# The excite of a dynamic convolution moved from TensorE to VectorE, in a two-layer convolution kernel

## The chip, the cores and the metric

The kernel runs on one core of a Trainium2 chip. The metric is the device time of one execution in microseconds, as the median of several runs. Before the change it is 3594.07 us (three runs, 3593.32 to 3596.56).

## What is computed

The input x is 16 images of 192 channels and 64 by 64 pixels, in fp32. A first layer (a layer norm, projections, depthwise convolutions, scans in four directions, a batch norm over all images, and a two-layer perceptron with residuals) gives an image of the same shape. The second layer, which the change is about, takes a mean of every channel, works four convolution taps per image and channel out of these means, and applies them:

```python
def _L1_conv_ref(x, w1, gamma, beta, running_mean, running_var, w2, b2, bias):
    ...
    b, c, h, w = x.shape
    pooled = x.mean(axis=(2, 3))
    t = pooled @ w1.T
    t = gamma * (t - running_mean) * jax.lax.rsqrt(running_var + EPS) + beta
    t = jax.nn.relu(t)
    wt = t @ w2.T + b2
    wt = wt.reshape(b * DIM, 1, K, K) * jnp.tile(MASK, (b, 1, 1, 1))
    out = jax.lax.conv_general_dilated(x.reshape(1, b * c, h, w), wt, window_strides=(1, 1), padding=((1, 1), (1, 1)), feature_group_count=b * DIM, dimension_numbers=('NCHW', 'OIHW', 'NCHW'))
    out = out + jnp.tile(bias, (b,))[None, :, None, None]
    return out.reshape(b, c, h, w)
```

`pooled @ w1.T` (192 to 48 values), the normalisation and the relu are called the squeeze here, `t @ w2.T + b2` (48 values to taps) the excite. The mask leaves four of the nine taps.

## The kernel before

The program writes the order of each engine's instructions out by hand: an engine works its instructions in the order in which the Python calls them, and waits where a tile that it needs isn't ready. It has three stages.

The first stage (lines 250 to 595) norms and projects the pixels, 64 chunks of 9.4 us on TensorE. Small jobs are hung on single chunks with `beside(n, ...)`: chunks 40 to 44 load weights (`load_weights`, among them `w1t` and `w2t`, the weights of squeeze and excite), and chunk 50 runs `squeeze_scale`, which works out the factor `s1` of the normalisation and divides `w1t` by the number of pixels.

The second stage (lines 598 to 806) runs over pairs of channels: `depthwise`, `scans`, `local`, `vertical`, `gate`. Its loop begins at k = −2; there TensorE first does `hidden_bias` (line 141: 18 products with one column, tile `pb_h`) and then `depthwise(0)` (line 629, tile `ps_d`). The tile `stats` takes the batch-norm sums from `gate(0)` on, and nothing uses it earlier.

The third stage (lines 810 to 1376) takes two images at a time, a pair, in 8 chunks of 512 pixels: 64 iterations of the loop at line 1256. Of 128 partitions the first 64 hold the one image and the others the other, with the 192 channels in three groups t of 64. In an iteration, TensorE does the first layer of the perceptron of chunk n (`first`, line 996), the means and the output projection for later chunks (`mean`, `out_quarters`, `out_columns`, lines 935, 899, 906), and the second layer (`second`, `seven`, `last_tile`, with line 851 for all their products). VectorE adds the results to the image (`residual`, `onto`), ScalarE does the activations, GpSimd the sums of operands that `seven` needs (`differences`).

Where a pair has ended (`ended`, the first iteration of the next pair, eight times in all), the taps are worked out: `pooled` adds the channel sums up (line 1109), `squeeze` multiplies them with `w1t` on TensorE (line 1115, tile `ps_t`: 48 partitions, one column per image) and normalises on VectorE (lines 1117 and 1118), and `excite` makes the taps with 24 products of one column each (through `both`, line 851, tile `ps_k`) and adds b2 on VectorE (line 1128). `squeeze` is called between the two halves of the output projection, `excite` between two steps of `second`. From the next lines on, `begin` and `piece` apply the taps: the first on ScalarE (line 1138), three on VectorE (line 65), in pieces spread over the next pair's iterations. After the last pair there is nothing to spread them over: squeeze, excite, diagonal matrices of the taps (line 1348), and the convolution on TensorE, ScalarE and VectorE at once (`dynamic_last`) follow each other.

PSUM is handed out in pools: `f1` (two tiles of two banks), `f2` (three of one bank) and `a` (one bank). `ps_t` is of `f1`, `ps_k` of `a`, the accumulators of `second` are of `f2` and `f1`.

Of the kernel before, what the change touches and what calls it, by code (L numbers as in the profile page):

```python
# [31 lines left out]
CH = 512  # L32
# [4 lines left out]
NG = HW // GR  # L37
NFC = 6
RED = 48
NTAP = 4  # L40
# [15 lines left out]
def conv_block_kernel(ctx: ExitStack, tc: tile.TileContext, x, prm, w_in, w_out, w_fc1, b_fc1, w_fc2, w1, bn1, w2, out):  # L56
    nc = tc.nc
    n_img_all = x.shape[0]
    n_pairs = n_img_all // 2
# [3 lines left out]
    HALF = (slice(0, 64), slice(64, 128))  # L63
# [23 lines left out]
    pt3 = cp.tile([128, 3, NPRM], F32, tag="pt3", name="pt3")  # L87
    eps5 = cp.tile([128, 1], F32, tag="eps5", name="eps5")
    eps6 = cp.tile([128, 1], F32, tag="eps6", name="eps6")
    ident = cp.tile([128, 128], F32, tag="ident", name="ident")  # L90


    k2 = ctx.enter_context(tc.tile_pool(name="k2", bufs=1))
# [6 lines left out]
    wf2 = place[:, 0:NFC * C].rearrange("p (m c) -> p m c", m=NFC)  # L100
    bf1 = k2.tile([128, NFC], F32, tag="bf1", name="bf1")
    w1t = k2.tile([128, 3, RED], F32, tag="w1t", name="w1t")
    w2t = k2.tile([RED, NTAP, C], F32, tag="w2t", name="w2t")
    b1 = k2.tile([RED, 4], F32, tag="b1", name="b1")
    s1 = k2.tile([RED, 1], F32, tag="s1", name="s1")

    mean64 = k2.tile([128, 64], F32, tag="mean64", name="mean64")

# [22 lines left out]
    def squeeze_scale():  # L131
        nc.scalar.activation(s1, b1[:, 3:4], AF.Sqrt, bias=eps5[0:RED])
        nc.vector.reciprocal(s1, s1)
        nc.vector.tensor_mul(s1, s1, b1[:, 0:1])

        nc.vector.tensor_scalar_mul(w1t, w1t, 1.0 / NPIX)

    def hidden_bias(pb):
        for m in range(NFC):
            for t in range(3):  # L140
                nc.tensor.matmul(pb[:, m:m + 1], wf1[0:64, t, 128 * m:128 * m + 128],  # L141
                                 pt3[0:64, t, LN2B:LN2B + 1], start=(t == 0), stop=(t == 2))
        nc.vector.tensor_add(bf1, bf1, pb[:, 0:NFC])
# [18 lines left out]
    ce = early.enter_context(tc.tile_pool(name="early", bufs=1))  # L162

    SB_ = 2 * 2 * C * BR
    mid = ce.tile([128, SB_], F32, tag="mid", name="mid")
    ones = ce.tile([128, 128], F32, tag="ones", name="ones")
    pv = ce.tile([128, 2, NPRM], F32, tag="pv", name="pv")


# [1 line left out]
    dec_b = ce.tile([128, 2, C // 2], F32, tag="dec_b", name="dec_b")  # L171
    bias_q = ce.tile([128, 3, C // 2], F32, tag="bias_q", name="bias_q")
    stats = ce.tile([128, C, 6], F32, tag="stats", name="stats")

    mask = ce.tile([128, 2, 1, HW], F32, tag="mask", name="mask")

# [73 lines left out]
    with ExitStack() as stage:  # L250
# [291 lines left out]
        for dst, src in ((pt3, prm), (w0, w_in)):  # L542
            v = src.rearrange("(t p) n -> p t n", p=64)
# [54 lines left out]
    with ExitStack() as stage:  # L598
# [168 lines left out]
        for k in range(-2, n_bp + 1):  # L767
            if 0 <= k + 1 < n_bp:
                tables(k + 1)
            if k >= 1:  # L770
                vertical(k - 1)
                gate(k - 1)
                g, c = divmod(k, hp_)
                if c == 0 and 0 < g < NCG - 1:
                    load_lm(g + 1)
                if c == 0 and g == 3:
                    load_weights(2)
                if c == 0 and g + 2 < NCG:
                    load_pg(g + 2)
                if c == hp_ - 2 and g + 2 < NCG:  # L780
                    load_dm(g + 2)
            if 0 <= k + 1 < n_bp:
                scans(k + 1)
            if k == -2:
                hidden_bias(psb.tile([128, 2, CH], F32, tag="l", name="pb_h")[:, 0])
            if k + 2 < n_bp:
                depthwise(k + 2)
            if 0 <= k < n_bp:
                local(k)
                sigmoid(k)  # L790
            if k in (1, 3, 5):
                scale_hidden(k // 2)
            if k == n_bp - hp_:

                load_y(0, y_low, (nc.sync,), (0, 1))
                load_x2(0)
                load_x2(1)
            if k == n_bp - hp_ // 2:
                load_y(0, y_low, (nc.sync,), (2,), LASTC)
# [48 lines left out]
    def both(ps, w, rhs, start, stop, **kw):  # L848

        for i, q in enumerate(HALF):  # L850
            nc.tensor.matmul(ps[q], w(i), rhs(i), start=start, stop=stop, **kw)  # L851
# [259 lines left out]
    def squeeze(p):  # L1111
        s = pst[p]
        pt = ps2.tile([128, 2, CH], F32, tag="f1", name="ps_t", bufs=2)[:, 0]
        for t in range(3):
            nc.tensor.matmul(pt[0:RED, 0:2], w1t[:, t], pool2[:, t], start=(t == 0), stop=(t == 2))
        red = hp2.tile([RED, 2], F32, tag="red2", name="red2")
        nc.vector.tensor_scalar(red, pt[0:RED, 0:2], b1[:, 2:3], s1, ALU.subtract, ALU.mult)
        nc.vector.tensor_scalar(red, red, b1[:, 1:2], 0.0, ALU.add, ALU.max)
        s["red"] = red

    def excite(p):
        s = pst[p]
        pk = ps2.tile([128, 3, NTAP, 1], F32, tag="a", name="ps_k")
        for t in range(3):
            for k in range(NTAP):
                both(pk[:, t, k], lambda i: w2t[:, k, 64 * t:64 * t + 64], lambda i: s["red"][:, i:i + 1], True, True)
        taps = hp2.tile([128, 3, NTAP], F32, tag="taps", name="taps")
        nc.vector.tensor_add(taps, pk[:, :, :, 0], pt3[:, :, B2:B2 + NTAP])
        s["taps"] = taps

    def dynamic(p, g, t):
# [124 lines left out]
    for n in range(n_ch + 1):  # L1256
        p, c = divmod(n, NCH)
        ended = p - 1 if n and c == 0 else None
        at(final, n - 1)
        if ended is not None:  # L1260
            pooled(ended)
            if ended == n_pairs - 1:
                idle(1)
        if n == 0:
            nc.vector.memset(pool2, 0.0)
        if n == 1:
            load_y(6, ys[3], (nc.sync,))
# [36 lines left out]
        at(first, n, NPS + 2)  # L1304
        at(differences, n, 2, 2)
        po = []
        if n + 2 < n_ch:

            own = [ps2.tile([128, CH], F32, tag="f2", name="ps_o1", bufs=3)[:, 0:HCH],
                   ps2.tile([128, CH], F32, tag="a", name="ps_o1")[:, 0:HCH]]  # L1310
            pair = ps2.tile([128, 2, CH], F32, tag="f1", name="ps_o", bufs=2)
            po = [[pair[:, wh, 0:HCH] for wh in range(2)], own, [pair[:, wh, HCH:CH] for wh in range(2)]]
            out_quarters(n + 2, 1, po[1], True)
        if n + 1 < n_ch:
            st[n + 1]["pw"] = two_banks("ps_v")
            mean(n + 1, st[n + 1]["pw"], "sq")
        at(load, n + 3)
        if po:
            for t in (0, 2):
                out_quarters(n + 2, t, po[t], True, t < 2)  # L1320
        if ended is not None:
            squeeze(ended)
        if po:
            for t in (1, 0, 2):
                out_columns(n + 2, t, po[t], False, t > 0)
            residual(n + 2, 1, po[1])
        at(spread_root, n + 1)
        steps = second(n) if n < n_ch else iter(())
        next(steps, None)
        at(scale, n + 1)  # L1330
        if po:
            for t in (0, 2):
                residual(n + 2, t, po[t])
        next(steps, None)
        at(bn_gelu, n + 3)
        if ended is not None:
            excite(ended)
            if ended < n_pairs - 1:
                pieces += [(ended, g, t) for g in range(NG) for t in range(3)]
        next(steps, None)  # L1340
        begin(2 if c % 2 == 0 or n == n_ch - 3 else 1)
        next(steps, None)
# [76 lines left out]
```

## The time and the profile before

| | |
|---|---|
| median of 3 runs | 3594.07 us |
| time of the profiled execution | 3596.65 us |
| its span (first to last instruction) | 3594.9 us |
| mean granted TensorE clock | 0.997 |
| TensorE busy | 3572.8 us (99% of the span) |
| VectorE busy | 2748.3 us (76%) |
| ScalarE busy | 1836.6 us (51%) |
| GpSimd busy | 1156.2 us (32%) |
| squeeze on TensorE (ps_t), records | 48 |
| excite on TensorE (ps_k), records | 384 |

The profile is one execution on the chip. Its page has the busy time of each engine, the chain of work that ended last (followed back from the last instruction, at each step to what released it), and the costliest groups of instructions. PE stands for TensorE's products, PEld for its weight loads, DVE for VectorE, ACT for ScalarE, POOL for GpSimd, SP for SyncE's DMA queue. A line such as `ps_k L851` is the group of line 851 that writes the tile ps_k; `x48` counts records, of which an fp32 product leaves two. Idle time is given in square brackets with what ended it. The span leaves 1.75 us of the profiled execution's time outside.

### The profile page before, as it was taken

How to read it: one execution, taken by the hardware profiler on the slowest of the kernel's cores; microseconds unless marked ns; L12 is line 12 of the kernel's file. 1: busy time of each engine (PE TensorE's matmuls, PEld its weight loads, DVE VectorE, ACT ScalarE, POOL GpSimd, SP SyncE). 2: the span in 40 equal slices, each digit the busy share in tenths (PEclk: the TensorE clock that was granted, in tenths of full speed). 3: DMA queues.
4: the chain of work that ended last, by engine and by line, in shares of the span. 5: the costliest groups of instructions: out<-in, count | busy, mean ns of one | idle time of the engine just before them, and what ended most of it. 6: DMA issues, size and time to landing. Idle time of an engine off the chain costs nothing.

```text
span 3594.9 us, 77663 instructions
## 1 busy us (share of the span) xinstructions
PE 3572.8 (99%) x32658; PEld 1885.2 (52%) x32658; DVE 2748.3 (76%) x4722; ACT 1836.6 (51%) x2067; POOL 1156.2 (32%) x1246
## 2 busy tenths in 40 slices
PE   9999999999999999999999999999999999999998
PEld 6666666555566654445444444445444444444443
DVE  6878777899999985556777777677777767777765
ACT  3443334888888863434444453444445444444533
POOL 3434332111111123433333343433333343333433
PEclk9999999999999999999999999999999999999999
DMA  7898998999999961112222222222222222222213
GB/s 165 240 257 254 258 271 242 301 301 283 281 283 286 281 143 41 45 44 72 60 68 75 65 74 61 79 60 68 73 66 74 61 79 60 69 75 65 74 34 89
DMA packets 288981, 492.19 MB, mean 137 GB/s; under 512 B 24816, under 2 KB 183016, under 8 KB 288632
## 3 DMA queue, kind: packets, MB, share of 16 engines
q1 hardware_dynamic: 246772, 341.85, 35.5%
q0 software_dynamic: 40928, 144.36, 14.1%
q8 instruction: 257, 4.21, 0.5%
q10 hardware_dynamic: 932, 1.03, 0.1%
q14 instruction: 92, 0.75, 0.1%
HBM read 284.95 MB, written 197.92 MB: 134 GB/s over the span
## 4 chain that ended last, share of the span: by engine, by line
PE 90%; DVE 1%; DMA 1%; issue 0%; ACT 0%; ACTq 0%; SPq 0%; POOL 0%; DVEq 0%
PE ps_f L996 28%; PE ps_f L851 18%; PE ps_l L673 11%; PE ps_pj L514 8%; PE ps_d L629 7%; PE ps_s L851 7%; PE ps_o L906 5%; PE ps_o L899 2%; PE ps_xt L485 1%; PE ps_m L935 1%; PE ps_v L935 1%; PE ps_k L851 0%; DMA xa<-in_x_dram 0%; DVE o L65 0%; PE pb_h L141 0%
## 5 line engine op out<-in xcount | busy, mean ns | idle before, releaser
L996 PE MATMUL ps_f<-h,wf 64*64 64x512 f32 x9216 | 1015.0, 591 | 0.0
L998 ACT ACTIVATE gl<-ps_f,bf 128x1024 f32<-128x1024 f32 x384 | 427.9, 1114 | 1082.0 <-PE ps_f L996 1079.7
L996 PEld LDWEIGHTS ps_f<-h,wf 64*64 64x64 f32 x9216 | 346.9, 133 | 598.4 <-issue 574.6
L851 PE MATMUL ps_f<-gl,place 128*64 128x256 f32 (+1 forms) x3072 | 528.7, 486 | 1.1 <-ACT rs L978 1.1
L514 PE MATMUL ps_pj<-wi,xa 64*128 64x384 f32 x3072 | 516.1, 488 | 1.6 <-DVE mid L519 1.0
L514 PEld LDWEIGHTS ps_pj<-wi,xa 64*128 64x128 f32 x3072 | 292.8, 188 | 196.4 <-issue 11.6
L1031 POOL TENSOR_TENSOR gl<-gl 128x512 f32<-128x512 f32 x192 | 308.8, 1635 | 159.1 <-PE ps_f L851 159.1
L851 PEld LDWEIGHTS ps_f<-gl,place 128*64 128x64 f32 x3072 | 225.5, 137 | 217.4 <-issue 145.7
L1021 POOL COPY turn<-o 128x1 f32<-128x1 f32 x84 | 16.4, 195 | 832.8 <-DVE o L65 832.8
L1027 POOL TENSOR_TENSOR t<-gl 128x512 f32<-128x512 f32 x192 | 246.1, 1282 | 89.1 <-ACT gl L998 44.7
L1029 POOL TENSOR_TENSOR t<-gl,t 128x512 f32<-128x512 f32 x192 | 247.1, 1287 | 44.2 <-ACT gl L998 30.7
L473 POOL DMA_DIRECT2D xa<-in_x_dram x192 | 120.4, 635 | 362.5 <-PE ps_pj L514 319.8
L65 DVE SCALAR_TENSOR_TENSOR o<-ximg,taps,o 128x1024 f32<-128x1024 f32 x180 | 231.7, 1288 | 4.9
L664 DVE TENSOR_TENSOR_SCAN v<-tab,q 128x1024 f32<-128x1024 f32 x96 | 218.3, 2274 | 7.8 <-ACT tab L652 7.8
L666 DVE TENSOR_TENSOR_SCAN v<-tab,q 128x1024 f32<-128x1024 f32 x96 | 217.5, 2266 | 0.0
L520 ACT ACTIVATE mid<-ps_pj,rsa 128x384 f32<-128x384 f32 x128 | 120.3, 941 | 184.9 <-PE ps_pj L514 178.6
L520 ACT ACTIVATE stg<-ps_pj,rsa 128x384 f32<-128x384 f32 x128 | 120.3, 941 | 180.6 <-PE ps_pj L514 176.3
L1054 DVE SCALAR_TENSOR_TENSOR ximg<-ps_f,pt,ximg 128x256 f32<-128x256 f32 (+1 forms) x176 | 96.6, 549 | 151.2 <-PE ps_f L851 151.2
L652 ACT ACTIVATE tab<-mask,dec_b 128x1024 f32<-128x1024 f32 x192 | 209.8, 1146 | 0.0
L492 DVE BATCH_NORM_STATS2 st<-ps_xt 128x6 f32<-128x192 f32 x512 | 173.1, 338 | 15.6 <-PE ps_xt L485 14.8
L912 DVE SCALAR_TENSOR_TENSOR ximg<-ps_o,pt,low 128x256 f32<-128x256 f32 x264 | 113.1, 479 | 92.9 <-PE ps_o L906 90.2
L906 PE MATMUL ps_o<-low,wo 128*64 128x256 f32 x1536 | 182.1, 385 | 0.4 <-ACT low L879 0.4
(258 smaller groups left out, 5686.0 us busy)
## 6 DMA issues: line engine op xcount, KB each, us to landing
low<-in_x_dram SPq DMA_DIRECT2D x128, 384.0 KB
out_dram<-o SPq DMA_DIRECT2D x172, 256.0 KB
mid<-pg_d SPq DMA_DIRECT2D x8, 4096.0 KB
low<-mixed_d SPq DMA_DIRECT2D x116, 256.0 KB
low<-pg_d SPq DMA_DIRECT2D x7, 4096.0 KB
pg_o<-pg_d SPq DMA_DIRECT2D x7, 4096.0 KB
xa<-in_x_dram POOLq DMA_DIRECT2D x192, 128.0 KB, 5.6
xa<-in_x_dram SPq DMA_DIRECT2D x192, 128.0 KB
```

Of the source, the lines that this page charges most:

```text
L65: nc.vector.scalar_tensor_tensor(o, in0, scalar, in1, ALU.mult, ALU.add, **kw)
L514: nc.tensor.matmul(ps[i], pixels(n, t, g)[q], wi[q, t].rearrange("p g k c -> p (g k c)"), start=(t == 0), stop=(t == 2))
L520: nc.scalar.activation(stag[blk][1][:, :, j], ps[1], AF.Copy, scale=rs[:, g, 1:2])
L629: nc.tensor.matmul(dst(ps[o, ih]), mats[g % 2]["dm"][q, di + 1, :, ch], src(s["pg"][q, :, 0, ch]), start=(di == 0), stop=stop)
L673: nc.tensor.matmul(dst(bst[k]["ps"][o, i]), lm_of(g)[q, m, :, c], src(q, ih), start=start, stop=stop)
L851: nc.tensor.matmul(ps[q], w(i), rhs(i), start=start, stop=stop, **kw)
L906: nc.tensor.matmul(ps[wh][q].rearrange("p (r w) -> p r w", w=32), wo[:, 64 * t:64 * t + 64], cols(rows(s["mx"][:, i]))[:, :, wh], start=fi ...
L996: nc.tensor.matmul(pf[o, i], wf1[q, t, m0:m0 + 64], s["h"][q, t], start=(t == 0), stop=(t == 2))
L998: nc.scalar.activation(gl, pf, AF.Gelu, bias=bf1[:, m:m + 1])
L1027: sub(t1[:, m], b12(m), b11(m))
L1029: sub(t2[:, m], b22(m), t1[:, m])
L1031: sub(b12(m), b22(m), b12(m))
```

## The change

The squeeze is turned round. Before, `w1t` was the stationary operand and the result stood on 48 partitions. Now the image's pooled column, repeated 64 times by a broadcast, is stationary and `w1t` with its 48 columns is the moving operand: every one of the 64 partitions of an image gets the whole row of 48 squeezed values. With the row in every partition, the excite is a product and a sum along the free dimension, which VectorE does: one instruction takes the maximum with 0 and multiplies by `w2x` (12 taps of 48 weights for the channel of each partition), one reduces the 48, and one adds b2. `excite` and its 24 products are gone, and the taps are made within `squeeze`.

For this, `w2t` has to stand by channel. `taps_by_channel` turns it once, with 24 products against the identity matrix, ahead of `depthwise(0)`; `squeeze_rows` folds the factor `s1` into `w1t` and makes the row of constants `c0`, with one product that spreads two rows over all partitions. Four small VectorE instructions in `squeeze_scale` prepare its operand. `w2t` itself now lies in the memory of `stats`.

```diff
@@ -134,6 +135,28 @@
         nc.vector.tensor_scalar_mul(w1t, w1t, 1.0 / NPIX)
+        nc.vector.tensor_mul(sq_s, b1[:, 2:3], s1)
+        nc.vector.tensor_sub(sq_s, b1[:, 1:2], sq_s)
+        for k, v in enumerate((s1, sq_s)):
+            nc.vector.tensor_scalar_mul(sq_d[:, k], ident[0:RED, 0:RED], v)
+
+    def squeeze_rows(pr):
+
+        nc.tensor.matmul(pr[:, 0:2 * RED], ones[0:RED], sq_d.rearrange("p k r -> p (k r)"), start=True, stop=True)
+        nc.vector.tensor_mul(w1t, w1t, pr[:, 0:RED].unsqueeze(1).broadcast_to([128, 3, RED]))
+        nc.vector.tensor_copy(c0, pr[:, RED:2 * RED])
+
+    def taps_by_channel(pk):
+
+        for t in range(3):
+            for k in range(NTAP):
+                j = (2 * t + k % 2) * RED
+                for q in HALF:
+                    nc.tensor.matmul(pk[q, k // 2, j:j + RED], w2t[:, k, 64 * t:64 * t + 64], ident[0:RED, 0:RED],
+                                     start=True, stop=True)
+        for h in range(2):
+            nc.scalar.activation(w2x[:, :, 2 * h:2 * h + 2], pk[:, h, 0:6 * RED].rearrange("p (t k r) -> p t k r", t=3, r=RED),
+                                 AF.Copy)
...
+    w2t = stats[0:RED].rearrange("p c e -> p (c e)")[:, 0:NTAP * C].rearrange("p (k c) -> p k c", k=NTAP)
...
@@ -783,6 +809,8 @@
             if k == -2:
                 hidden_bias(psb.tile([128, 2, CH], F32, tag="l", name="pb_h")[:, 0])
+                taps_by_channel(psb.tile([128, 2, CH], F32, tag="l", name="pk_h"))
+                squeeze_rows(psb.tile([128, 2, CH], F32, tag="d", name="pr_h", bufs=2)[:, 0])
             if k + 2 < n_bp:
                 depthwise(k + 2)
@@ -1112,20 +1140,16 @@
         s = pst[p]
         pt = ps2.tile([128, 2, CH], F32, tag="f1", name="ps_t", bufs=2)[:, 0]
         for t in range(3):
-            nc.tensor.matmul(pt[0:RED, 0:2], w1t[:, t], pool2[:, t], start=(t == 0), stop=(t == 2))
-        red = hp2.tile([RED, 2], F32, tag="red2", name="red2")
-        nc.vector.tensor_scalar(red, pt[0:RED, 0:2], b1[:, 2:3], s1, ALU.subtract, ALU.mult)
-        nc.vector.tensor_scalar(red, red, b1[:, 1:2], 0.0, ALU.add, ALU.max)
-        s["red"] = red
-
-    def excite(p):
-        s = pst[p]
-        pk = ps2.tile([128, 3, NTAP, 1], F32, tag="a", name="ps_k")
-        for t in range(3):
-            for k in range(NTAP):
-                both(pk[:, t, k], lambda i: w2t[:, k, 64 * t:64 * t + 64], lambda i: s["red"][:, i:i + 1], True, True)
+            for i, q in enumerate(HALF):
+                nc.tensor.matmul(pt[q, 0:RED], pool2[q, t, i:i + 1].broadcast_to([64, 64]), w1t[q, t], start=(t == 0), stop=(t == 2))
+        red = hp2.tile([128, RED], F32, tag="red2", name="red2")
+        nc.vector.tensor_add(red, pt[:, 0:RED], c0)
+        prod = hp2.tile([128, 3, NTAP, RED], F32, tag="prod", name="prod", bufs=1)
+        flat = lambda a: a.rearrange("p t k r -> p (t k) r")
+        nc.vector.scalar_tensor_tensor(flat(prod), red.unsqueeze(1).broadcast_to([128, 3 * NTAP, RED]), 0.0, flat(w2x), ALU.max, ALU.mult)
         taps = hp2.tile([128, 3, NTAP], F32, tag="taps", name="taps")
-        nc.vector.tensor_add(taps, pk[:, :, :, 0], pt3[:, :, B2:B2 + NTAP])
+        nc.vector.tensor_reduce(taps.rearrange("p t k -> p (t k)"), flat(prod), AX.X, ALU.add)
+        nc.vector.tensor_add(taps, taps, pt3[:, :, B2:B2 + NTAP])
         s["taps"] = taps
@@ -1333,10 +1357,8 @@
         at(bn_gelu, n + 3)
-        if ended is not None:
-            excite(ended)
-            if ended < n_pairs - 1:
-                pieces += [(ended, g, t) for g in range(NG) for t in range(3)]
+        if ended is not None and ended < n_pairs - 1:
+            pieces += [(ended, g, t) for g in range(NG) for t in range(3)]
         next(steps, None)
```

More of the change, by code (lines that the diff above doesn't have):

```diff
@@ L102, in conv_block_kernel @@
     w1t = k2.tile([128, 3, RED], F32, tag="w1t", name="w1t")
-    w2t = k2.tile([RED, NTAP, C], F32, tag="w2t", name="w2t")
     b1 = k2.tile([RED, 4], F32, tag="b1", name="b1")
     s1 = k2.tile([RED, 1], F32, tag="s1", name="s1")
+    w2x = k2.tile([128, 3, NTAP, RED], F32, tag="w2x", name="w2x")
+    c0 = k2.tile([128, RED], F32, tag="c0", name="c0")
     mean64 = k2.tile([128, 64], F32, tag="mean64", name="mean64")
@@ L166, in conv_block_kernel @@
     ones = ce.tile([128, 128], F32, tag="ones", name="ones")
+    sq_s = ce.tile([RED, 1], F32, tag="sq_s", name="sq_s")
+    sq_d = ce.tile([RED, 2, RED], F32, tag="sq_d", name="sq_d")
     pv = ce.tile([128, 2, NPRM], F32, tag="pv", name="pv")
```

## The prediction

> **What bounds the kernel now.** I read the page first (busy shares, then the chain that ended last), then the chain by time around the end of an image pair, then VectorE's timeline there, the windows at the start of the second stage, and the chain at the very end.
>
> From the page, parts 1 and 4:
>
> ```profile
> PE 3572.8 (99%) x32658; PEld 1885.2 (52%) x32658; DVE 2748.3 (76%) x4722; ACT 1836.6 (51%) x2067; POOL 1156.2 (32%) x1246
> ...
> PE 90%; DVE 1%; DMA 1%; issue 0%; ACT 0%; ACTq 0%; SPq 0%; POOL 0%; DVEq 0%
> ```
>
> TensorE is busy for the whole span and carries nine tenths of the chain; what TensorE does not have to do comes off the time one for one, unless somebody else then arrives late. The chain in order of time gives the price of the edited place:
>
> ```profile
> 1571.13 5.31 PE ps_f L996 x48
> ...
> 1605.86 5.31 PE ps_f L996 x48
> ...
> 1642.49 5.31 PE ps_f L996 x48
> ...
> 1677.22 5.31 PE ps_f L996 x48
> ```
>
> The columns are start, length, what. An ordinary iteration of the third stage starts 34.73 us after the one before (1605.86 − 1571.13, 1677.22 − 1642.49). The one that ends a pair takes 36.63: 1.90 more, and the same at the other six pair ends (1885.57 to 1922.20, and so on). Inside it:
>
> ```profile
> 1623.63 0.31 PE ps_t L1115 x5
> ...
> 1630.50 1.49 PE ps_k L851 x48
> 1631.99 1.45 PE ps_s L851 x12
> ```
>
> The excite is the 1.49, and the group behind it takes 1.45 where groups of that shape take 1.29 elsewhere in the chain: 1.65 in all. The remaining 0.25 is the squeeze. VectorE in the same stretch (start, length, line, and in brackets the idle time before it and who ended it):
>
> ```profile
> 1624.03 0.27 DVE L1117 TENSOR_SCALAR red<-ps_t,b,s 48x2 f32<-48x2 f32 x1 [4.71 <-PE ps_t L1115]
> 1624.33 0.22 DVE L1118 TENSOR_SCALAR red<-red,b 48x2 f32<-48x2 f32 x1
> 1624.53 0.92 DVE L912 SCALAR_TENSOR_TENSOR spare<-ps_o,pt,low 128x256 f32<-128x256 f32 x2
> 1625.41 0.10 DVE L1065 MEMSET sums<- 128x48 f32 x1
> 1627.98 0.49 DVE L1054 SCALAR_TENSOR_TENSOR spare<-ps_f,pt,spare 128x256 f32<-128x256 f32 x1 [2.48 <-PE ps_f L851]
> ```
>
> It is waiting for TensorE on both sides of the place where the new work goes. Windows at the start of the second stage (stretch, its length, busy time and records of each engine, the granted TensorE clock, DMA share, GB/s):
>
> ```profile
> 629.50:632.90 3.40, 3.36 (x30) 3.37 (x31) 0.00 (x0) 0.00 (x0) 3.10 (x6) 1.00 0.49 120
> 632.90:636.30 3.40, 3.40 (x20) 2.17 (x23) 0.16 (x1) 0.00 (x0) 0.00 (x0) 0.50 0.98 300
> 636.30:639.70 3.40, 3.40 (x36) 1.79 (x32) 0.00 (x0) 0.00 (x0) 0.67 (x1) 0.50 1.08 382
> 639.70:643.10 3.40, 3.40 (x52) 1.99 (x48) 0.71 (x1) 3.34 (x5) 0.26 (x1) 1.00 1.11 372
> ```
>
> After 4.8 us of one-column products (pb_h, 629.54 to 634.33) the clock is at half for 6.8 us, and ps_d, which follows without a gap, runs in that. The change puts more small products exactly there. Last, the end of the kernel, from the chain:
>
> ```profile
> 3557.67 0.41 PE ps_t L1115 x6
> ...
> 3558.11 0.28 DVE red L1117
> ...
> 3558.41 0.23 DVE red L1118
> ...
> 3558.78 1.58 PE ps_k L851 x48
> ...
> 3560.38 0.18 DVE taps L1128
> ```
>
> Here nothing lies beside squeeze and excite: from 3557.67 to 3560.56 they are the chain, 2.89 us.
>
> [...]ps_t's records start 45 ns apart, the pairs of ps_k (both column halves) 58, pb_h's 112; at half clock pb_h's are 214 apart. So these little products cost weight loads and not columns.[...]
>
> **The change, part by part.** Each fp32 product leaves two records (24 instructions, 48 records of ps_k).
>
> (a) Excite gone from TensorE at seven pair ends inside the loop: −1.65 each. Nothing else of those iterations moves on TensorE, so a pair end becomes an ordinary iteration plus a squeeze. Ordinary iterations show that the rest (GpSimd's differences, the PSUM banks, the residuals) keeps up at 34.73.
>
> (b) Squeeze: 3 products of 48 weight columns become 6 of 64 (12 records) on two tiles of the array that share neither rows nor columns. ps_k's two tiles share rows and still ran in pairs at 58 to 62 ns, so six pairs are 0.37 us, where the old six records took 6 × 0.045 = 0.27: +0.10. The 48 moving columns are some 41 ns a record, by ps_f's 512 columns in 442 ns per tile (four tiles, a record every 110.6), and lie under the loads. Bounds: +0 if the pairs start as early as before, +0.47 if all 12 loads come one after another. I take +0.10, since every shape on disjoint tiles in this trace overlaps. Net of (a) and (b): −1.55 each, seven times −10.9; ends −8.3 and −11.6.
>
> (c) VectorE at a pair end: out go 0.27, 0.22 and, later, 0.17 (taps); in come an add of 48 from PSUM (between L1128's 170 and L1117's 270 ns: 0.21), a scalar_tensor_tensor of 576 (L1054's 746 ns at 512 plus 64 × 1.06, the slope to L65's 1288 at 1024: 0.81), a reduce of 576 (199 + 528 × 1.04: 0.75) and a 12-wide add (0.17), with three handovers of 0.03: 2.05 us, 1.55 more ahead of residual(1). It starts at the same place, 4.71 us idle (3.4 at the other pair ends) lie before it, and the 2.48 us idle before L1054 takes the 1.55. Behind the block wait two residuals, the memset and L1054. residual(1)'s PSUM banks are next written in the following iteration: the second product's first groups take the two banks that ScalarE has read (ps_v's), so TensorE does not wait for the block. Up to the store after ps_s (L1054 again), VectorE had 2.48 + 0.34 + 1.28 = 4.10 idle; TensorE comes 1.65 sooner and the block is 1.4 longer in sum, so about 1 us is left. Cost 0; without that cover, the excess over 1 us, seven times. GpSimd can stretch VectorE (L961 has a mean of 1238 ns where the same shape takes 692), but its next work, L1031, starts at 1628.88, after the block.
>
> (d) ScalarE: its two first dynamic activations waited 3.00 us for taps; they now start at 1629.25 without it. ScalarE isn't next in line: 0.
>
> (e) First stage: four VectorE instructions of at most 48 columns (0.15 to 0.2 us each, by L133 and L134) after the old three at 509.5. The next VectorE wait there is 0.89 us; they fit: 0, or up to 0.3 if not.
>
> (f) Ahead of the second stage: 24 products and one more (48 + 2 records) between pb_h and ps_d. At full clock 24 pairs × 0.06 + 2 × 0.11 = 1.65 us; at half clock, as here, 3.3. Beside nothing: ps_d is on the chain and waits for pb_h alone. In this trace ps_d would start at 637.6. If the clock opens at 639.7 as before, the loss in full-speed work is 1.65; if the window up to 639.7 isn't busy enough (the one before, 60% full of ps_d, was not), it opens 3.4 us later, at half the work: 3.35. I take 2.4, between[...]. ScalarE's two copies (288 columns, about 0.5 us each by L642's 1.11 at 1024) and VectorE's two reads fall where both were idle over 7 us: 0. The w2t load stays where it was on SP's queue; no DMA issue moves on any queue.
>
> (g) The end: 12 records (0.36, and 0.18 for the last to land) plus VectorE's 2.05 and hand-overs of 0.06 are 2.65 against 2.89: −0.25. The half-clock window that follows there (3561.5 to 3564.9) lies on a free-running grid, so ±0.65 more.
>
> Sum: −10.9 − 0.25 + 2.4 = −8.75 us. The profiled execution has a span of 3594.9 us and a time of 3596.65, 1.75 outside it, which stays; it lies 2.6 (0.07%) above the median of 3594.07. The sum off the median: 3585.3.
>
> **Rivals.**
> *R1, half the gain*: the 12 loads don't overlap (−8.3), the clock opens a window late (+3.35), the end loses 0.65 − 0.25: −4.6, 3589.5. For it: the window of 632.9 that was 60% full and did not open the clock; against: ps_k's overlap.
> *R2, no gain at the pair ends*: another engine sets the 36.6 and only (f) and (g) remain: +2.15, 3596.2. For it: VectorE's margin of 1 us is thin; against: TensorE never waits in the pair-end chain.
> *R3, slower*: the VectorE block holds up TensorE. Place: behind it L1054, which empties the bank that the next group adds to. Price: all of the block above 2.05 + 1, seven times. Break-even at (8.75/7 = 1.25) a block of 4.3 us; slower by 0.2% from 5.3. At 5.6 us: +17.9 − 8.75, 3603.2. For it: L961's stretch of 1.8, but applied to both wide instructions that makes a block of 3.3 and costs only 2. Something unseen about the broadcast operand would have to come on top.
> That the change doesn't take the excite off TensorE can be left out: its 24 products per pair are not in the new order.
>
> **How the numbers follow.** Chances: forecast 0.71, R1 0.16, R2 0.06, R3 0.07. The forecast's own range runs from −11.6 − 0.9 + 1.65 = −10.9 (3583.2) to −10.15 + 0.4 + 3.35 = −6.4 (3587.7: the squeeze at +0.2, the clock a window late). R1 belongs in the range; runs of the kernel before differ by up to 3 us. So 3582.5 to 3590.5. A measurement of this kernel tells about 0.2%, 7.2 us, from no change: the line is 3586.9. The forecast lies 1.6 beyond it, so about nine tenths of it counts as faster, with a sliver of R1: 0.66. The rest of both and R2: 0.27. R3: 0.07.
>
> **What would show it.** Right: iterations at pair ends of about 35.1 us; ps_t with 12 records in some 0.4; L1054 still waiting for TensorE about 1 us; ps_d first at about 636 to 637.6. Wrong: pair ends over 35.5; an idle TensorE there released by VectorE; a clock at 0.50 beyond 640 at the second stage.

## The result and the profile after

| | before | after |
|---|---|---|
| median of 9 runs | 3594.97 us | 3584.55 us |
| lowest to highest | 3592.60 to 3597.15 | 3581.80 to 3587.28 |
| time of the profiled execution | 3596.65 | 3587.28 |
| its span | 3594.9 | 3585.5 |

The ratio is 0.9971, with a 95% interval of 0.9961 to 0.9982: the change makes the kernel faster, by 0.18 to 0.39%. The prediction said 3585.3, which was a change of −8.75 us from the median of three runs that it had (3594.07); over nine runs of each kernel the medians differ by 10.4. Both profiled executions are slower than their kernel's median, by 1.7 and 2.7 us, so the profiles below differ by less, 9.4 us.

From the page of the kernel after, part 1 (busy time, share of the span, records):

```profile
PE 3561.8 (99%) x32372; PEld 1946.5 (54%) x32372; DVE 2758.7 (77%) x4736; ACT 1836.0 (51%) x2069; POOL 1155.9 (32%) x1246
```

TensorE has 11.0 us less to do and VectorE 10.4 more, while TensorE still fills the span. The chain in order of time, around the same pair end as before (start, length, what):

```profile
1574.14 5.31 PE ps_f L1024 x48
...
1608.87 5.31 PE ps_f L1024 x48
...
1626.64 0.33 PE ps_t L1144 x12
1626.97 2.74 PE ps_o L934 x24
...
1643.93 5.31 PE ps_f L1024 x48
...
1678.65 5.31 PE ps_f L1024 x48
```

An ordinary iteration still takes 34.73 (1574.14 to 1608.87, 1643.93 to 1678.65). The one at the pair end takes 35.06 in place of 36.63, and what remains above an ordinary one is exactly the squeeze, 0.33. The same holds at all seven. VectorE there (start, length, line and instruction, idle time before it and who ended that):

```profile
1627.01 0.21 DVE L1146 TENSOR_TENSOR red<-ps_t,c 128x48 f32<-128x48 f32 x1 [4.68 <-PE ps_t L1144]
1627.25 0.87 DVE L1149 SCALAR_TENSOR_TENSOR prod<-red,w2x 128x576 f32<-128x576 f32 x1
1628.16 0.75 DVE L1151 TENSOR_REDUCE taps<-prod 128x12 f32<-128x576 f32 x1
1628.94 0.17 DVE L1152 TENSOR_TENSOR taps<-taps,pt 128x12 f32<-128x12 f32 x1
...
1631.06 0.49 DVE L1082 SCALAR_TENSOR_TENSOR spare<-ps_f,pt,spare 128x256 f32<-128x256 f32 x1 [1.06 <-PE ps_f L879]
...
1634.93 0.48 DVE L1082 SCALAR_TENSOR_TENSOR spare<-ps_s,pt,spare 128x256 f32<-128x256 f32 x1 [0.15 <-PE ps_s L879]
```

The new block takes 2.10 us (1627.01 to 1629.11), and VectorE still waits for TensorE after it, 1.06 and 0.15 us.

At the start of the second stage, the windows of the clock's grid as the trace shows it (3.41 us each, laid out from the moments at which the granted clock changes), with TensorE's busy time on ps_d alone in the second number, then records, the granted clock, the DMA share and GB/s:

```profile
629.01:632.42 3.41, 0.00 (x0) 1.00 0.63 142
632.42:635.83 3.41, 0.00 (x0) 0.50 0.96 291
635.83:639.25 3.42, 2.45 (x16) 0.50 1.08 379
639.25:642.66 3.41, 3.41 (x36) 0.50 1.11 368
642.66:646.07 3.41, 3.41 (x52) 1.00 1.02 415
```

The grid is read from these moments alone: in the profile of before they are 15.08, 18.49, 632.89, 639.72, 1308.73, 1312.14, 3561.53 and 3564.94, which are 1, 180, 2, 196, 1, 659 and 1 times 3.413 us apart; in the profile of after 14.61, 18.02, 632.42, 642.66, 1311.67 and 1315.09, which are 1, 180, 3, 196 and 1 times that.

Three windows run at half clock, where the kernel before had two. The end, from the chain:

```profile
3549.59 0.56 PE ps_t L1144 x11
3550.16 2.44 issue
3552.60 1.99 PE ps_d L1190 x32
```

Squeeze and taps take 3.01 us here (3549.59 to 3552.60), and the first ps_d group 1.99. Before it was 3.32 (3557.61 to 3560.93) and 3.18:

```profile
3560.93 3.18 PE ps_d L1166 x32
```

The two spans differ by 9.4 us. Cut at the same places, the difference divides as follows:

| stretch | before | after | difference |
|---|---|---|---|
| start to the end of the last projection | 628.55 | 627.88 | −0.67 |
| from there to the first product of the third stage | 699.51 | 703.19 | +3.68 |
| third stage to the last squeeze (seven pair ends) | 2229.55 | 2218.52 | −11.03 |
| last squeeze to the end of the first ps_d group | 6.50 | 5.00 | −1.50 |
| the rest | 30.79 | 30.91 | +0.12 |

The pair ends came as predicted. The second and the fourth line of the table are larger than predicted, with opposite signs, and the experiments look at them.

### The profile page after: what moved, and what is told of

Read it like the earlier page. It is cut to its first block, busy times and chain, and to the rows that moved or that the text cites. A ratio compares the mean times of both kernels' runs of the same rounds, so it can differ in the third digit from the quotient of the medians.

```text
span 3585.5 us, 77114 instructions
## 1 busy us (share of the span) xinstructions
PE 3561.8 (99%) x32372; PEld 1946.5 (54%) x32372; DVE 2758.7 (77%) x4736; ACT 1836.0 (51%) x2069; POOL 1155.9 (32%) x1246
## 4 chain that ended last, share of the span: by engine, by line
PE 90%; DVE 1%; DMA 1%; issue 0%; ACT 0%; ACTq 0%; POOL 0%; SPq 0%
PE ps_f L1024 28%; PE ps_f L879 18%; PE ps_l L699 11%; PE ps_pj L540 8%; PE ps_d L655 7%; PE ps_s L879 7%; PE ps_o L934 5%; PE ps_o L927 2%; PE ps_xt L511 1%; PE ps_m L963 1%; PE ps_v L963 1%; DVE o L65 0%; DMA xa<-in_x_dram 0%; PE pb_h L164 0%; DVE ol L65 0%
## 5 line engine op out<-in xcount | busy, mean ns | idle before, releaser
L1059 POOL TENSOR_TENSOR gl<-gl 128x512 f32<-128x512 f32 x192 | 308.5, 1633 | 159.8 <-PE ps_f L879 159.8
```

What stands on the lines that cost most here:

```text
L1059: sub(b12(m), b22(m), b12(m))
```

## The experiments

Ten kernels, each compared with runs of the kernel before on the chip on which it ran. On the three chips used the kernel before took 3594.53, 3595.76 and 3595.47 us, so kernels of different chips are compared by their ratios to it. Each diff is against the kernel after unless it says otherwise; `...` marks what is left out.

**The preparation alone.** Against the kernel before: only what stands ahead of the second stage is added (with the constants it reads), and its results are written where nothing reads them.

```diff
...
             if k == -2:
                 hidden_bias(psb.tile([128, 2, CH], F32, tag="l", name="pb_h")[:, 0])
+                taps_by_channel(psb.tile([128, 2, CH], F32, tag="l", name="pk_h"))
+                squeeze_rows(psb.tile([128, 2, CH], F32, tag="d", name="pr_h", bufs=2)[:, 0])
```

> The kernel before with the preparation alone: the four small VectorE instructions, the 24 turning products, the product of the rows and their reads, with results that nothing uses; squeeze and excite in the third stage stay as before. Theory: it costs 1.7 us plus 1.7 for each extra window at half clock, so 1.7 to 3.4 us (3.4 in the profile of the changed kernel), and pair ends stay at 36.63. Rival (the preparation is hidden and the changed kernel's gain at the pair ends is smaller than read off): no change from before within 0.5 us.

Measured: 3598.40 us (13 runs) against 3594.53 (18 runs), ratio 1.0012 (1.0004 to 1.0021). That is 3.9 us, with 1.4 to 7.5 as the interval; some 0.4 of it lies outside the span (2.2 us in this kernel, 1.8 in the kernel before). Pair ends stay at 36.63. From its chain:

```profile
629.42 4.97 PE pb_h L163 x36
634.40 2.73 PE pk_h L154 x48
637.13 0.67 PE pr_h L144 x2
637.79 10.46 PE ps_d L658 x116
```

pk_h and pr_h take 3.40 us, at half clock (1.85 at full clock, in the next experiment), and three windows are at half. The span is 3.4 longer than the one of before. The rival, no cost, is out. The whole gain of the change thus sits at the pair ends and the end, and the preparation takes back some three tenths of it (3.7 of 12.5 us in the table above).

**The preparation in the first stage.** `taps_by_channel`, in two halves, and `squeeze_rows` are hung on chunks 52, 54 and 56.

```diff
...
         beside(50, squeeze_scale)
+        for h in range(2):
+            beside(52 + 2 * h, lambda h_: taps_by_channel(bank(), h_), h)
+        beside(56, lambda: squeeze_rows(bank()))
...
                 hidden_bias(psb.tile([128, 2, CH], F32, tag="l", name="pb_h")[:, 0])
-                taps_by_channel(psb.tile([128, 2, CH], F32, tag="l", name="pk_h"))
-                squeeze_rows(psb.tile([128, 2, CH], F32, tag="d", name="pr_h", bufs=2)[:, 0])
```

> The changed kernel with the 24 turning products and the product of the squeeze rows moved into the first stage (chunks 52, 54 and 56), where TensorE is dense. Theory (small products cost their weight loads, and more at half clock): they cost about 1.7 us there at full clock instead of the 3.4 us that the changed kernel lost ahead of ps_d, the low-clock stretch at the second stage's start is two windows again and not three, and the time is 1.5 to 2 us under the changed kernel's, about 12 us under before. Rival (what is lost there is a wait, for the DMA that brings pg or for a PSUM bank, and not TensorE's work): ps_d then starts no sooner than in the changed kernel, and the time is higher than the changed kernel's by the 1.7 us.

Measured: 3583.81 us (5 runs), ratio 0.9966 (0.9952 to 0.9979). From its chain:

```profile
527.94 0.83 PE pb L155 x24
...
547.57 0.83 PE pb L155 x24
...
567.21 0.19 PE pb L145 x2
...
632.65 4.80 PE pb_h L163 x36
637.45 2.56 PE ps_d L657 x10
```

In the first stage the same products cost 1.85 us (0.83 + 0.83 + 0.19), at full clock but not beside anything: they stand in the chain there too. In front of ps_d they are gone, two windows are at half clock again, and from the last projection to the third stage it takes 699.7 us, as before the change. So the move exchanges 3.7 for 1.85. The rival, a wait for a transfer or a bank, is out: ps_d starts 5.9 us after the last projection in place of 9.0. The time is 10.7 under the kernel before, short of the expected 12 but inside the interval; the kernel after, 0.7 us away, can't be told from it.

**How the clock sets the price.** With the same preparation at the same place, the traces differ. For each kernel: when the last projection ends, when ps_d starts, how many windows are at half clock, and the time from the last projection to the first product of the third stage.

| kernel | projection ends | ps_d starts | windows | to stage 3 |
|---|---|---|---|---|
| before | 628.55 | 634.33 | 2 | 699.5 |
| preparation in stage 1 | 631.59 | 637.45 | 2 | 699.7 |
| after, block doubled (below) | 623.18 | 632.10 | 2 | 701.2 |
| after, one half after the other (below) | 623.98 | 634.54 | 3 | 702.8 |
| before with the preparation | 628.36 | 637.79 | 3 | 703.0 |
| after | 627.88 | 636.87 | 3 | 703.2 |
| after, block tripled (below) | 626.80 | 637.71 | 4 | 704.7 |
| after, product twice, reduce three times (below) | 623.67 | 634.53 | 4 | 704.7 |

The six with the preparation here lie 1.7, 3.3, 3.5, 3.7, 5.2 and 5.2 us above the kernel before: 1.7 for the products, and 1.7, half a window, for every window beyond two. The six have the same products at this place and the grid elsewhere against them. Each line is one execution, so the table shows what can occur and not how often. In the kernel with the doubled block (columns as in the windows above), a ps_d that filled 2.77 of a window opened the clock with the next one:

```profile
627.97:631.38 3.41, 0.00 (x0) 0.50 0.93 289
631.38:634.80 3.42, 2.77 (x16) 0.50 1.08 378
634.80:638.21 3.41, 3.41 (x60) 1.00 1.10 375
```

In the kernel after, 2.45 of 3.42 didn't. Over six of the eight kernels (before, after, the doubled and the tripled block, one half after the other, product twice), the windows that ps_d filled for 2.73 and 2.77 opened it, and those that it filled for 1.98 to 2.45 did not.

**One half after the other.** The six squeeze products in another order, so that neighbours share the tile of the array.

```diff
-        for t in range(3):
-            for i, q in enumerate(HALF):
+        for i, q in enumerate(HALF):
+            for t in range(3):
```

> The changed kernel with the six squeeze products in another order: the three of the first 64 partitions, then the three of the others, so that neighbours share a tile of the array. Theory[...]: the 12 records of ps_t take about 0.65 to 0.7 us instead of 0.33 and pair ends about 35.4 instead of 35.06. Rival ([...]the loads never overlapped): ps_t stays at 0.33 us.

One run: 3585.48 us. ps_t takes 0.47 and the pair ends 35.20 (1604.60 to 1639.80), 0.14 more than in the kernel after:

```profile
1604.60 5.31 PE ps_f L1024 x48
...
1622.37 0.47 PE ps_t L1144 x12
...
1639.80 5.29 PE ps_f L1024 x45
```

The direction is that expected (with neighbours on different tiles the twelve records take 0.33, in this order 0.47), the size under half of it: 0.14 where 0.32 to 0.37 was put. So the records still overlap in part in this order too; how is not shown.

**The VectorE block, doubled.** Product and reduce run twice at the seven pair ends.

```diff
-        nc.vector.tensor_reduce(taps.rearrange("p t k -> p (t k)"), flat(prod), AX.X, ALU.add)
+        for again in range(2):
+            if again and p < n_pairs - 1:
+                nc.vector.scalar_tensor_tensor(flat(prod), red.unsqueeze(1).broadcast_to([128, 3 * NTAP, RED]), 0.0, flat(w2x), ALU.max, ALU.mult)
+            if again == 0 or p < n_pairs - 1:
+                nc.vector.tensor_reduce(taps.rearrange("p t k -> p (t k)"), flat(prod), AX.X, ALU.add)
```

> The changed kernel with the product and the reduce of the VectorE block done twice at the seven pair ends inside the loop, not at the last (the result is the same). The block grows by some 1.65 us to 3.7. Theory (VectorE has 1.06 us idle behind the block and 0.15 before the next store, 1.2 in all): pair ends take 0.4 to 0.5 us more than 35.06, 3 us in all, and the 1.06 us of idle time is gone. Rival 1 (the block is wholly hidden, since TensorE needs VectorE only much later): pair ends stay at 35.06. Rival 2 (TensorE waits for all of the block): pair ends take 1.65 us more, 11.5 us in all, which eats the gain.

Measured: 3585.33 us (5 runs), ratio 0.9969 (0.9957 to 0.9981), and every pair end at 35.06:

```profile
1602.21 5.31 PE ps_f L1024 x48
...
1637.27 5.31 PE ps_f L1024 x48
```

The theory was wrong and the rival of no cost right. 1.58 us more of VectorE went in where its idle time ahead of the two stores was 1.06 and 0.15. So that idle time is not the whole room, and the next two runs measure the rest.

**The block tripled**, in the same way with `range(3)`.

> The product and the reduce run three times at the seven pair ends, so the VectorE block is about 5.2 us in place of 2.0; the two repeats compute nothing new. Theory (the prediction's break-even of 4.3 us of block): TensorE is held for about 1 us at each pair end, which becomes 36.0 to 36.1 us in place of 35.06; the span grows by 7. Rival A (the doubled block, 3.7 us, cost nothing at all, and the banks bridge this one too): pair ends stay at 35.06, and only idle time of VectorE is used up. Rival B (no cover left after the doubled block): each pair end grows by the whole 1.5 us, to 36.6.

One run: 3607.85 us, span 3606.1. Five pair ends take 37.24 (or 37.23), two 38.93 and 38.94; the kernel before had 36.63. Here TensorE waits, for the store of line 1082 that empties the bank of the next ps_s. TensorE's, GpSimd's and VectorE's timeline at one of the seven:

```profile
1920.55 1.52 PE L879 MATMUL ps_s<-gl,place 128*64 128x256 f32 x12 [1.96 <-DVE ximg L1082]
```
```profile
1914.38 5.28 POOL L1059 TENSOR_TENSOR gl<-gl 128x512 f32<-128x512 f32 x3 [4.45 <-PE ps_f L879]
```
```profile
1914.53 1.15 DVE L1156 TENSOR_TENSOR taps<-taps,pt 128x12 f32<-128x12 f32 x1
...
1916.79 1.74 DVE L1014 TENSOR_TENSOR h<-h,rs 128x1536 f32<-128x1536 f32 x1
```

Two things add up. The add of b2, 12 elements wide, took 1.15 us in place of 0.17, starting 0.15 us after GpSimd had begun. And at the two longest pair ends TensorE's pause dropped the clock, for one window. All three expectations missed: the holding is real, and each pair end grew by 2.18 us or more.

**Product twice, reduce three times**, a block between the two, to separate them: `if again == 1 and p < n_pairs - 1` on the product, `range(3)`.

> The product runs twice and the reduce three times at the seven pair ends; the repeats compute nothing new. The VectorE block is then about 4.4 us without handovers stretched (doubled: 3.6, tripled: 5.2 and one add that took 1.15 in place of 0.17). Theory: the add of b2 starts before GpSimd's next work and takes 0.17 again, so the block lies between the two others; the doubled block left about 0.55 us of room ahead of the store after ps_s, so that TensorE waits 0.2 to 0.3 us at each pair end and these become 35.2 to 35.4 us (35.06 doubled, 37.24 tripled). Rival (the add is slow because the block has grown, not because GpSimd is at work): it takes over 1 us again and the pair ends are 36.2 to 36.5.

One run: 3591.30 us, pair ends at 35.97 to 35.99. The add takes 0.17 again, as the theory had it, and the rival is out; but the pair ends were put at 35.2 to 35.4. VectorE, GpSimd and TensorE at one pair end:

```profile
1628.62 0.17 DVE L1156 TENSOR_TENSOR taps<-taps,pt 128x12 f32<-128x12 f32 x1
...
1629.93 2.23 DVE L1014 TENSOR_TENSOR h<-h,rs 128x1536 f32<-128x1536 f32 x1
```
```profile
1629.27 5.27 POOL L1059 TENSOR_TENSOR gl<-gl 128x512 f32<-128x512 f32 x3 [4.46 <-PE ps_f L879]
```
```profile
1634.18 1.52 PE L879 MATMUL ps_s<-gl,place 128*64 128x256 f32 x12 [0.69 <-DVE spare L1082]
```

But another instruction met GpSimd: the product on `h` (1536 elements) took 2.23 in place of 1.75. With that, the room can be worked out. The extra reduce and its handover are 0.79 and the stretch 0.48, together 1.27, of which TensorE saw 0.69: 0.58 was left behind the doubled block, and 1.58 + 0.58 = 2.16 behind the change's own. The tripled block checks it: 2 × 1.58 + 0.98 of stretch, less 2.16, is 1.98, and the wait was 1.96. The pair end grows by another 0.22 or 0.23 beyond the wait. Most of this isn't a further cost: without a wait TensorE's groups overlap in the records (in the doubled kernel ps_s starts at 1629.35, 0.17 before the group ahead of it ends), so counted from start to start the room is nearer 2.0.

**The hidden bias in the first stage too.** As the kernel with the preparation in stage 1, with `beside(58, lambda: hidden_bias(bank()))` in place of the call at k = −2.

> The taps, the squeeze rows and the hidden bias are all worked out in the first stage, so that TensorE has nothing to do between the last projection and the first ps_d. Theory (in the kernel after, these products stand in front of ps_d, and only the landing of the four low<-mid transfers is behind them): ps_d starts 4.1 to 4.4 us after the last projection, in place of 8.97; the first stage grows by 1.85 (measured) and by 3.5 to 4.1 for the bias, so that the whole is within 2 us of the kernel after. The clock still drops to half, since the gap is idle. Rival (the transfers land later, and the products cost nothing where they stand): ps_d starts 8 to 9 us after the last projection and the kernel is 5 us slower than after.

One run: 3594.13 us, and neither theory holds as a whole. ps_d does start early: its first four records 1.10 us after the last projection (634.02), the others, after a wait of 2.12 for low<-mid, 4.36 us after it. But the next two groups of channels then wait for transfers that are still under way: 0.71 us for pg_d<-mid at 660.07, and 2.19 for dm<-dv_d at 690.13, a pause that costs a further window at half clock. And in the first stage the bias's one-column products took 3.91 us and dropped the clock there, for the window that begins at 587.9.

**Wide products in the gap.** As that kernel, with eight 512-column products at k = −2, ahead of the second stage, and four at the end of the third; what they compute is not used. The diff is against that kernel.

```diff
...
+            if k == -2:
+                pb_h = psb.tile([128, 2, CH], F32, tag="l", name="pb_h")
+                for _ in range(8):
+                    nc.tensor.matmul(pb_h[:, 0], ident, wf1[:, 0, 0:CH], start=True, stop=True)
...
             squeeze(ended)
+            if ended == n_pairs - 1:
+                idle(4)
```

> As the kernel with everything turned in the first stage, and TensorE runs eight 512-column products, whose result is not used, from the last projection to the first ps_d, and four at the end of the third stage while VectorE works out the last taps. Theory (products of 48 columns or one column count as idle for the clock, wide ones as busy): no window at half clock at the start of stage 2 and none before the last ps_d; the start of stage 3 is 1.5 to 3.5 us earlier than in the kernel after, the end another 0 to 1.4; 3579 to 3583 us. Rival (the clock drops whatever runs in the gap): half clock for two or three windows, 3585 to 3588.

Measured: 3590.85 us (21 runs), ratio 0.9988 (0.9981 to 0.9994). The clock is as the theory had it: no window at half clock at the start of the second stage (the first ps_d group of the chain takes 8.09 us, in the kernel before 10.65), none before the last ps_d (1.93 us). The price was not: a product took 0.89 us, so the eight held ps_d up by 3.5 us and the four held the end up by 1.2. The profiled execution, 3586.53 us, is the fastest of the 21; that the clock held in the others as well is not shown.

**Four and two of them.**

> As the kernel with eight wide products in the gap ahead of the second stage and four at the end, with four and two in their place: each turned out to take 0.89 us[...], so that eight held the first ps_d up by 3.5 us and four the last one by 1.2. Theory: the first ps_d starts 4.4 to 4.8 us after the last projection (8.2 with eight), the last one 2.44 us after the last squeeze (3.6 with four), both at full clock, and the time is 4 to 5 us below the 3590.85 of that kernel: 3586 to 3587, which is no better than the kernel after, because the bias and the taps still take 5.9 us of TensorE in the first stage. Rival (the clock, not the length of the filler, set that kernel's time, and four products are too few to keep it up): half clock at the start of stage 2 and 3588 to 3591.

Measured: 3589.87 us (13 runs), ratio 0.9986 (0.9978 to 0.9995). The clock stays up (the first 120 records of ps_d take 8.16 us, in the kernel before 10.72; the last group takes 2.00), ps_d starts 4.7 us after the last projection, and the last one 2.4 after the squeeze. The ratio to the kernel before is the same within the intervals (0.9986 and 0.9988), where 4 to 5 us were expected. TensorE's only wait from 655 to 665 us, where ps_d goes over to the next group of channels (line, what it waited for, us in total, times, the longest):

```profile
PE ps_d L658 <- DMA pg_d<-mid: 2.2, 1, 2.2
```

and the first stage where the bias now stands (windows of the grid; length, then busy time of TensorE, weight loads, VectorE, ScalarE, GpSimd, the clock, DMA share, GB/s):

```profile
585.97:589.38 3.41, 3.41 (x18) 3.40 (x18) 0.16 (x1) 0.00 (x0) 1.58 (x3) 0.50 1.04 312
589.38:592.80 3.42, 3.42 (x14) 2.51 (x14) 0.98 (x4) 0.00 (x0) 0.00 (x0) 0.50 0.86 290
```

In this execution, what is gained at the border of the stages is lost twice: ps_d runs into the transfers, 2.2 us, and the one-column products now drop the clock in the middle of the first stage, for two windows.

**The preparation in the first stage and the end kept warm.** The second experiment, with `idle(4)` behind the last squeeze.

> The taps and the squeeze rows turned in the first stage, the hidden bias left ahead of the second, and four 512-column products, whose result is not used, at the end of the third stage between the last squeeze and the last ps_d. Theory: the start of stage 2 as in the kernel with the taps turned in stage 1 (two windows at half clock, stage 1 longer by 1.85), and the last 32 products of ps_d always take 1.99 us, never 3.35; the four products[...] fit into the 2.44 us in which TensorE waits there. 0.3 to 1 us under that kernel's 3583.8. Rival (the four products hold the last ps_d up, or the clock drops all the same): the wait of 2.44 becomes 3 or more, or ps_d takes 3.35; no gain or 0.5 slower.

Measured: 3585.22 us (7 runs), ratio 0.9973 (0.9962 to 0.9984). The last ps_d takes 1.93, but the four products take 3.63 where 2.44 were free: 1.2 lost for 1.36 that is saved only where half clock would have fallen. No gain, as the rival said.

No version beats the kernel after by more than a measurement can tell.

## Why the prediction was right, and where its terms were off

*The pair ends, (a) and (b).* Predicted −1.55 each, measured −1.57. The excite's whole price in the chain came off, and the squeeze costs 0.33 against 0.25. The products on two tiles do overlap: the twelve records take 0.33 us where neighbours are on different tiles, and 0.47 in the other order. No run takes away the excite alone, so the parts are read from the chain; their sum is measured.

*VectorE at the pair ends, (c).* Predicted 2.05 us of block, measured 2.10. The slope of 1.04 ns an element that the prediction took for the reduce was an estimate; by the profile of after, with 753 ns for 576 elements (L1151) and 199 for 48 (L1137), it is 1.05. Cost 0, as measured. The room was under-estimated: I put about 1 us, read from VectorE's idle time ahead of the stores; the runs show 2.16. VectorE may be late for its own store without anyone noticing (1.58 us more of it cost nothing in the doubled block), as long as TensorE is still filling another bank; what counts is when TensorE comes back to that bank. R3's mechanism exists: the tripled block makes the pair ends longer than before the change. Its break-even lies higher than the prediction's 4.3 us of block: that much (2.10 + 2.16 = 4.26 us of VectorE work, stretches by GpSimd counted in) is still about free, and the change's gain of 10.4/7 = 1.49 us per pair end is used up only some 1.27 later (1.49 less the 0.22), at an estimated 5.5.

*ScalarE, (d).* Its first dynamic activations, which had waited 3.00 us for the taps, now start without a wait, and the chain doesn't change, as predicted.

*The preparation in front of ps_d, (f): the term that was mis-sized.* The sum took 2.4, between 1.65 and 3.35. The profile of after shows 3.7 for that stretch, and six profiles 1.7 to 5.2, 3.8 in the mean; by its time alone the preparation costs 3.9 (1.4 to 7.5). The products themselves were put at 1.65 at full clock and took 1.85; the rest is the clock. Both of the prediction's ends occur, nearly, but its upper one is no bound: a fourth window at half clock is possible, and it was seen twice. A clock at 0.50 beyond 640 us, which the prediction had named as a sign of being wrong, was there in the profile of after (until 642.66); it is this term that it tells of. The 2.4 between the two ends was an estimate. The 48-column products opened no window: in the kernel with the doubled block they filled 2.68 of the window from 627.97 (the rest was pb_h), and the next window stayed at half, where 2.73 of ps_d opened it elsewhere. By the traces, 72% of one window filled with ps_d (2.45 of 3.42) was not enough to open the clock here, and 80% was (2.73 of 3.41).

*The end, (g).* Squeeze and taps: predicted −0.25, measured −0.31. The other −1.19 is the half-clock window that stood at 3561.5 before and is missing in the profile of after: TensorE's wait of 2.44 us was split by the grid over two windows, and the clock stayed up. That was luck: in the profiles of the doubled and the tripled block the clock dropped there again, and the first ps_d group took 3.35 and 3.66. The prediction allowed ±0.65 for that grid; downwards it should have been nearly twice that.

*The first stage, (e), and chance.* The first stage ended 0.67 us sooner. Its code is the same on either side but for the four small VectorE instructions of (e), and over the five kernels that have it as it is after the change it ended between 623.18 and 627.88: the profiles of after and of the tripled block, as that of before, have a window at half clock some 15 us after the start, the other three have none. So 0.67 says nothing of the change. The spread of 4.7 is about that of the nine runs of after (5.5).

So the forecast was met because its main term, seven pair ends, was right to 0.1 us, and, by luck, because two errors of the clock, +1.3 on (f) and −1.2 on the end, offset each other in the profile. The change itself came out larger by the medians (10.4 us) than forecast (8.75); that the level of 3585.3 is met within 0.8 owes something to the three runs that it started from, whose median was 0.9 below that of the nine.

## What to carry to other kernels

Where one engine carries the chain and the work repeats, price the edited iteration by its length in the chain against that of an ordinary one: that figure held to 0.02 us here. Idle time on the engine that takes the work over was only a lower bound of the room here (1.2 us idle, 2 us of room), and the rest was found at the buffer that the bound engine comes back to. Small products and pauses on TensorE should be priced by the clock windows that they cost behind them (1.7 us each here, ahead of ps_d), with a bound for the unluckiest position of the grid and not for the one that the profile happens to show.

## What the runs showed of the hardware

- Products of few moving columns went by the columns of their weights. At full clock, in the kernel before, a record of ps_t (48 columns of weights, two moving) came every 45 ns, a pair of ps_k (64 each, one moving) every 58 to 62, a record of pb_h (128, one moving) every 112. In the kernel after, the twelve records of ps_t with 64 columns of weights and 48 moving ones take 0.33 us, 55 ns a pair.
- Back-to-back products of one column keep TensorE busy by its records and can still drop the clock: 18 of them (3.9 us at full clock) in the first stage dropped it to half for one window in one kernel and for two in another, and left it alone in a third, where the grid split them in half (1.95 and 1.96 us in two windows; in the other two kernels 2.56 and 2.42 us fell into the window ahead of the drop).
- Pauses of TensorE of 1.96 us (two pair ends of the tripled block) and 2.19 us (the kernel with the bias in the first stage too) dropped the clock. Their windows had TensorE busy for 1.45 and 1.22 of 3.41 us. The same 1.96 us at the tripled block's other five pair ends, split by the grid, left it alone, once with 1.64 of 3.41 (2479.41 to 2482.82); so did the 2.44 us at the end of the kernel after (1.63 of 3.42, 3550.81 to 3554.23). At the start of the kernel with the preparation in stage 1 a window with 1.60 of 3.41 (11.36 to 14.77) lost the clock. Busy time alone doesn't tell: at the end of the kernel before, a window with 2.17 of 3.41 (3558.12 to 3561.53), 1.56 of it on the one-column products of ps_k, lost the clock too. What else counts stays open.
- Some VectorE instructions took longer where GpSimd was at work at the same time, a small one as well as a large one: the add of 12 elements took 1.15 in place of 0.17 where it started 0.15 us after one of GpSimd's L1059 (at both pair ends of the tripled block that were read in detail; its median over the eight is 1.15), the product of 1536 elements 2.23 in place of 1.75 where it started 0.66 after one, and the same add took 0.17 when it came before GpSimd's work. In the kernel before, L961 took 0.67 to 0.69 the 11 times that no GpSimd instruction overlapped it, and 1.33 to 1.43 the 52 times that one did. Where VectorE started first, GpSimd was the slower one: in the kernel after, the product of 1536 started at 1631.46 and took its usual 1.75, and the L1059 that started 0.50 later took 2.39 in place of 1.28.
